# Three transposes of each batch by 32x32 blocks on VectorE and moves by DMA, in a two-layer graph network

## Chip, cores and metric

One core of one Trainium2 chip. The metric is the device time of one execution in microseconds (us); a quoted time is the median of three or more executions unless the text says "one look". "Waits" and "half clock" come from the one profiled execution of each kernel.

## The reference, cut to what matters

Thirty-two batches, each with x (512x512), a weighted adjacency matrix (512x512) and a node mask (512), all in fp32.

```python
# layer 0
h = relu(layernorm(x))
agg = (adj @ h) / max(rowsum(adj), 1e-6)
x = x + relu(concat([h, agg], -1) @ W.T)
# layer 1
h = relu(layernorm(x))                       # "h1" in this text
q, k = split(h @ Wqk);  v = h @ Wv
w = scale * mask * sum(q * (adj @ (k * mask)), -1)
x = x + softmax(w)[:, None] * v
```

## The kernel before

Per batch it computes five products on TensorE: y = h W2, out = h W1 + A y (a double one), z = A (h1 masked), q = h1 M with M = Wq Wk^T, and v = h1 Wv. Each product of 512x512 matrices is done with seven products of halves instead of eight (a Strassen scheme), so the left and the right operand need a few sums first; the class `Left` makes those of the left operand. The kernel hands TensorE the left operand transposed, so h, the adjacency and h1 are each transposed once a batch, by TensorE against an identity, through PSUM, with a ScalarE copy back:

```python
class Left:                                  # sums of the left operand, on VectorE
    def __init__(self, t, name, tag):
        s = big.tile([P, 3, 2, H], F32, tag=tag, bufs=1, name=f"{name}_s")
        a11, a12, a21, a22 = block(t, 0, 0), block(t, 1, 0), block(t, 0, 1), block(t, 1, 1)
        s1, s2, s4 = s[:, 0], s[:, 1], s[:, 2]
        tt(s1, a21, a22, ALU.add)
        tt(a21, a11, a21, ALU.subtract)
        tt(s2, s1, a11, ALU.subtract)
        tt(s4, a12, s2, ALU.subtract)
        self.p = {1: a11, 2: a12, 3: s4, 4: a22, 5: s1, 6: s2, 7: a21}

def transpose_block(dst, src, c, func, name):
    p = ps_t.tile([P, 4, P], F32, tag="t", name=name)
    for d in range(4):
        nc.tensor.transpose(p[:, d, :], src[:, ts(d, P)], ident)
    nc.scalar.activation(dst[:, :, ts(c, P)], p, func)

def transpose_h1(b):                         # h and the adjacency alike
    t = tile4("h1T", 1, f"h1T_{b}")
    for c in range(C):
        transpose_block(t, XN[1, b][:, c, :], c, AF.Relu, f"pt1_{b}_{c}")
    H1T[b] = Left(t, f"h1T_{b}", "h1Ts")

# ... (layer_norm: statistics and the normalization on VectorE; the products; the softmax) ...

for i in range(B + 1):
    between = []
    if i < B:
        layer0_y(i)
    if i > 0:
        transpose_h1(i - 1)
        mask_h1(i - 1)
        XN.pop((1, i - 1))
        layer1_z(i - 1)
    if i < B:
        transpose_adj(i)
    if i + 1 < B:
        load_a(i + 1)
        XN[0, i + 1] = layer_norm(i + 1, f"0_{i + 1}")
    if i > 0:
        between = layer1_q(i - 1)
    if i < B:
        layer0_out(i, between)
    # ...
    if i + 1 < B:
        transpose_h(i + 1)
        normalize_adj(i + 1)
    if i > 0:
        layer1_v(i - 1)
    if i + 2 < B:
        load_x(i + 2)
```

The loop is the order of the program's text. The framework that builds the kernel puts instructions of one engine into an order of its own that keeps their dependences; once the kernel is built, these lists are fixed.

## Time and profile before

| | before |
|---|---|
| median of three executions | 2618.34 us (2617.97 to 2618.83) |
| TensorE's share of the chain that ended last | 97% |
| one batch, from one y to the next | 79.9 us |
| of it the three transposes on TensorE | 5.5 us |
| VectorE busy | 1647.6 us, 63% |
| DMA engines busy, data queue | 11.7% |
| granted TensorE clock, mean | 0.999 |

The share of the chain says whose time counts. Busy shares of the other engines are only room. One line that the prediction uses in words, from the list of waits (who waited for whom, us in total, times, longest):

```profile
PE pv L103 <- DVE u3v L64: 22.5, 31, 0.8
```

TensorE loses 0.75 us a batch at the start of a part of v, because VectorE is late with a sum that reads PSUM.

### The profile page before, as it was taken

The numbers are of one execution on the slowest core, as the hardware profiler recorded it, in microseconds if no ns is written. First come the engines' busy times: TensorE is split into PE (matmuls) and PEld (weight loads), VectorE is DVE, ScalarE is ACT, GpSimd is POOL, SyncE is SP. The second block draws the span as 40 slices with busy tenths as digits, with TensorE's granted clock in tenths as the row PEclk, the third lists the DMA queues.
The fourth block names the chain that finished last, engine by engine and source line by source line (L and its number), as shares of the span: only waits on it lengthen the run. The fifth ranks groups of instructions, "written<-read, shape, count | busy, mean of one in ns | idle before, by whom it ended". The sixth has DMA issues, their size and how long they took to land.

```text
span 2616.5 us, 30420 instructions
## 1 busy us (share of the span) xinstructions
PE 2559.3 (98%) x12548; PEld 2218.6 (85%) x12548; DVE 1647.6 (63%) x3282; ACT 481.6 (18%) x854; POOL 74.3 (3%) x70
## 2 busy tenths in 40 slices
PE   6999999999999999999999999999999999999998
PEld 4888888888888888888888888888888888888887
DVE  4766567666576665676665766656766657666555
ACT  2211212111121112121111211121211112111211
POOL 0000000000000000000000000000000000000000
PEclk9999999999999999999999999999999999999999
DMA  4100111010111000110101110011101011100000
GB/s 146 33 33 30 35 49 49 33 49 17 49 49 49 33 33 33 49 49 33 49 17 49 49 49 33 33 33 49 49 33 49 17 49 49 49 33 33 33 17 33
DMA packets 53514, 107.91 MB, mean 41 GB/s; under 512 B 1632, under 2 KB 1632, under 8 KB 53376
## 3 DMA queue, kind: packets, MB, share of 16 engines
q1 hardware_dynamic: 53376, 105.98, 11.7%
q8 instruction: 98, 1.61, 0.3%
q14 instruction: 40, 0.33, 0.0%
HBM read 72.42 MB, written 33.55 MB: 41 GB/s over the span
## 4 chain that ended last, share of the span: by engine, by line
PE 97%; DVE 1%; DMA 0%; SPq 0%; ACT 0%; issue 0%; POOL 0%; POOLq 0%; DVEq 0%
PE po L103 30%; PE pz L103 15%; PE pq L103 15%; PE pv L103 15%; PE py L103 15%; PE pth L154 2%; PE pta L154 2%; PE pt L154 2%; DVE u3v L64 1%; PE pm L339 1%; DMA mask_sb<-in_nodemask_dram 0%; PE pbc L297 0%; DVE st L202 0%; SPq L181 0%; PE psum L307 0%
## 5 line engine op out<-in xcount | busy, mean ns | idle before, releaser
L103 PE MATMUL po<-w1T,hT 128*128 128x256 f32 x768 | 200.5, 383 | 0.0
L103 PE MATMUL po<-y,aT 128*128 128x256 f32 x768 | 197.1, 379 | 0.0
L103 PE MATMUL pv<-wv_sb,h1T 128*128 128x256 f32 x768 | 186.7, 379 | 0.0
L103 PE MATMUL pq<-m_sb,h1T 128*128 128x256 f32 x768 | 186.6, 379 | 0.0
L103 PE MATMUL pz<-h1m,aT 128*128 128x256 f32 x768 | 186.6, 379 | 0.0
L103 PE MATMUL py<-w2T,hT 128*128 128x256 f32 x768 | 181.7, 379 | 0.7 <-ACT s1y L121 0.7
L202 DVE BATCH_NORM_STATS2 st<-x 128x6 f32<-128x512 f32 x256 | 166.8, 674 | 9.6 <-DMA x<-in_x_dram 8.1
L208 DVE TENSOR_SCALAR xn<-x,mv,rstd 128x512 f32<-128x512 f32 x256 | 122.6, 543 | 66.3 <-POOL rstd L205 66.3
L103 PEld LDWEIGHTS py<-w2T,hT 128*128 128x128 f32 x768 | 145.7, 190 | 21.3 <-ACT s1y L121 1.1
L103 PEld LDWEIGHTS po<-y,aT 128*128 128x128 f32 x768 | 145.9, 190 | 19.8
L103 PEld LDWEIGHTS po<-w1T,hT 128*128 128x128 f32 x768 | 143.2, 190 | 18.6
L103 PEld LDWEIGHTS pv<-wv_sb,h1T 128*128 128x128 f32 x768 | 141.2, 190 | 16.7
L103 PEld LDWEIGHTS pq<-m_sb,h1T 128*128 128x128 f32 x768 | 141.1, 190 | 16.6
L103 PEld LDWEIGHTS pz<-h1m,aT 128*128 128x128 f32 x768 | 141.0, 190 | 16.6
L205 POOL TENSOR_TENSOR rstd<-rstd,mhalf 128x4 f32<-128x4 f32 x64 | 73.6, 1151 | 2488.5 <-DVE rstd L204 2488.5
L64 DVE TENSOR_TENSOR pre<-po,u2o 128x512 f32<-128x512 f32 x64 | 44.3, 692 | 149.9 <-PE po L103 149.9
L103 PE MATMUL po<-w_t,hT_s 128*128 128x256 f32 x512 | 131.5, 379 | 0.0
L103 PE MATMUL po<-y_t,aT_s 128*128 128x256 f32 x512 | 131.4, 379 | 0.0
L155 ACT ACTIVATE hT<-pth 128x512 f32<-128x512 f32 x128 | 69.8, 595 | 334.5 <-PE pth L154 334.4
L103 PE MATMUL pv<-wv_t,h1T_s 128*128 128x256 f32 x512 | 121.1, 379 | 0.0
L103 PE MATMUL pz<-h1m_t,aT_s 128*128 128x256 f32 x512 | 121.0, 379 | 0.0
L103 PE MATMUL pq<-m_t,h1T_s 128*128 128x256 f32 x512 | 121.0, 379 | 0.0
(151 smaller groups left out, 4389.3 us busy)
## 6 DMA issues: line engine op xcount, KB each, us to landing
x<-in_x_dram SPq DMA_DIRECT2D x32, 1024.0 KB, 5.3
adj<-in_adj_dram SPq DMA_DIRECT2D x32, 1024.0 KB, 5.2
out_dram<-x SPq DMA_DIRECT2D x32, 1024.0 KB, 4.3
w_in<-in_L_gnn_W_dram SPq DMA_DIRECT2D x2, 1024.0 KB, 9.0
w_in<-in_L_gnn_Wqk_dram SPq DMA_DIRECT2D x2, 1024.0 KB, 13.1
wv_sb<-in_L_gnn_Wv_dram SPq DMA_DIRECT2D x1, 1024.0 KB, 14.4
mask_sb<-in_nodemask_dram SPq DMA_DIRECT2D x1, 64.0 KB, 12.0
```

The costliest lines, as they stand in the source:

```text
L64: nc.vector.tensor_tensor(o, a, b, op=op)
L103: nc.tensor.matmul(bank[:, rc, :], left.p[k][:, dc, ts(rc, P)], right.p[k][:, dc, :], start=(first and n == 0), stop=(n == 4 * len(pairs) ...
L154: nc.tensor.transpose(p[:, d, :], src[:, ts(d, P)], ident)
L155: nc.scalar.activation(dst[:, :, ts(c, P)], p, func)
L202: nc.vector.bn_stats(st, X[b][:, c, :])
L205: nc.gpsimd.tensor_tensor(rstd, rstd, mhalf, op=ALU.pow)
L208: nc.vector.tensor_scalar(xn[:, c, :], X[b][:, c, :], mv[:, c, 0:1], rstd[:, c:c + 1], op0=ALU.subtract, op1=ALU.mult,)
L339: nc.tensor.matmul(p, wqT[:, a, ts(d, P)], wkT[:, a, :], start=(a == 0), stop=(a == D - 1))
```

## The change

Its intent is to take all three transposes off TensorE, the engine that sets the end. VectorE transposes the 32x32 blocks of a matrix in place. That leaves each block in the wrong quadrant of 32 partitions, and 16 DMA transfers put them where they belong: each moves one source quadrant of partitions into one target quadrant, 32 partitions with 16 runs of 128 bytes, 64 KB. Each 128x128 block is turned where it stands, so the products index their left operand the other way round (not shown in the diff). ScalarE now does the normalization together with the relu. To make room, the results of q and v are no longer stored and are combined straight from PSUM. The transposed h gets two buffers.

```diff
+    def turn(t, src, name, how):
+        if how == "pe":
+            for c in range(C):
+                transpose_block(t[:, c, :].rearrange("p (d n) -> p d n", d=4), src[:, c, :], f"{name}_{c}")
+            return
+        for c in range(C):
+            nc.vector.transpose(src[:, c, :], src[:, c, :])
+        s16, t16 = (u.rearrange("p c (d n) -> p (c d) n", n=P) for u in (src, t))
+        for q in range(4):
+            for r in range(4):
+                nc.sync.dma_start(out=t16[ts(q, 32), :, ts(r, 32)], in_=s16[ts(r, 32), :, ts(q, 32)])
 # ... layer_norm:
-        xn = tile4("xn", 2, f"xn{name}")
+        nb = small.tile([P, C], F32, tag="nb", name=f"nb{name}")
+        nc.vector.scalar_tensor_tensor(nb, mv[:, :, 0], -1.0, rstd, op0=ALU.mult, op1=ALU.mult)
+        h = tile4("h", 2, f"h{name}")
         for c in range(C):
-            nc.vector.tensor_scalar(
-                xn[:, c, :], X[b][:, c, :], mv[:, c, 0:1], rstd[:, c:c + 1],
-                op0=ALU.subtract, op1=ALU.mult,
-            )
-        return xn
+            nc.scalar.activation(h[:, c, :], X[b][:, c, :], AF.Relu, bias=nb[:, c:c + 1], scale=rstd[:, c:c + 1])
+        return h
 # ... transpose_h:
-        t = tile4("hT", 1, f"hT_{b}")
+        t = tile4("hT", 2, f"hT_{b}")
+        turn(t, HN.pop((0, b)), f"pth_{b}", "dma")
+        HT[b] = Left(t, f"hT_{b}", "hTs", 2)
 # ... transpose_adj (one buffer still):
+        turn(t, A.pop(b), f"pta_{b}", "dma")
 # ... transpose_h1, now with the masking in it:
+        h = HN.pop((1, b))
+        hm = tile4("h1m", 1, f"h1m_{b}")
         for c in range(C):
+            nc.vector.tensor_scalar(hm[:, c, :], h[:, c, :], mcol[:, c, b:b + 1], None, op0=ALU.mult)
         t = tile4("h1T", 1, f"h1T_{b}")
+        turn(t, h, f"pt1_{b}", "dma")
+        H1M[b] = Right(hm, f"h1m_{b}", big, "h1mt")
+        H1T[b] = Left(t, f"h1T_{b}", "h1Ts")
 # ... q and v: products of PSUM pieces with z, or added to x, in half-width pieces;
 #     temporaries from two buffers to one, the tiles "c" from three to two
```

More of the change, by code (lines that the diff above doesn't have):

```diff
@@ L66, with __init__ @@
     class Left:
-        def __init__(self, t, name, tag):
-            s = big.tile([P, 3, 2, H], F32, tag=tag, bufs=1, name=f"{name}_s")
-            a11, a12, a21, a22 = block(t, 0, 0), block(t, 1, 0), block(t, 0, 1), block(t, 1, 1)
+        def __init__(self, t, name, tag, bufs=1):
+            s = big.tile([P, 3, 2, H], F32, tag=tag, bufs=bufs, name=f"{name}_s")
+            a11, a12, a21, a22 = block(t, 0, 0), block(t, 0, 1), block(t, 1, 0), block(t, 1, 1)
             s1, s2, s4 = s[:, 0], s[:, 1], s[:, 2]
@@ L103, in part @@
                         nc.tensor.matmul(
-                            bank[:, rc, :], left.p[k][:, dc, ts(rc, P)], right.p[k][:, dc, :],
+                            bank[:, rc, :], left.p[k][:, rc, ts(dc, P)], right.p[k][:, dc, :],
                             start=(first and n == 0), stop=(n == 4 * len(pairs) - 1),
@@ L123, in product @@
         part(6, p6, True)
-        u2 = temp("u2", 2)
+        u2 = temp("u2", 1)
         tt(u2, p6, s1, ALU.add)
@@ L127, in product @@
         part(7, p7, True)
-        u3 = temp("u3", 2)
+        u3 = temp("u3", 1)
         tt(u3, p7, u2, ALU.add)
@@ L148, in store_in, with transpose_block @@
         return sink
-    def transpose_block(dst, src, c, func, name):
+    def transpose_block(dst, src, name):
         p = ps_t.tile([P, 4, P], F32, tag="t", name=name)
@@ L154, in transpose_block @@
             nc.tensor.transpose(p[:, d, :], src[:, ts(d, P)], ident)
-        nc.scalar.activation(dst[:, :, ts(c, P)], p, func)
-    X, A, XN, HT, AT, Y, H1T, H1M, Z, DEGM, SM = ({} for _ in range(11))
+        nc.scalar.activation(dst, p, AF.Copy)
+    def turn(t, src, name, how):
[9 more added lines that the diff above has]
+                nc.sync.dma_start(out=t16[ts(q, 32), :, ts(r, 32)], in_=s16[ts(r, 32), :, ts(q, 32)])
+    X, A, HN, HT, AT, Y, H1T, H1M, Z, DEGM, SM = ({} for _ in range(11))
     def load_x(b):
@@ L177 @@
     for half, tag, bufs in (
-        (w0[:, 0:F], "x", 3), (w0[:, F:2 * F], "x", 3), (wqk[:, 0:F], "c", 3), (wqk[:, F:2 * F], "c", 3),
+        (w0[:, 0:F], "x", 3), (w0[:, F:2 * F], "x", 3), (wqk[:, 0:F], "c", 2), (wqk[:, F:2 * F], "c", 2),
     ):
@@ L225, in transpose_h @@
     def transpose_h(b):
-        t = tile4("hT", 1, f"hT_{b}")
-        xn = XN.pop((0, b))
-        for c in range(C):
-            transpose_block(t, xn[:, c, :], c, AF.Relu, f"pth_{b}_{c}")
-        HT[b] = Left(t, f"hT_{b}", "hTs")
+        t = tile4("hT", 2, f"hT_{b}")
+        turn(t, HN.pop((0, b)), f"pth_{b}", "dma")
+        HT[b] = Left(t, f"hT_{b}", "hTs", 2)
     def transpose_adj(b):
         t = tile4("aT", 1, f"aT_{b}")
-        an = A.pop(b)
-        for c in range(C):
-            transpose_block(t, an[:, c, :], c, AF.Copy, f"pta_{b}_{c}")
+        turn(t, A.pop(b), f"pta_{b}", "dma")
         AT[b] = Left(t, f"aT_{b}", "aTs")
     def transpose_h1(b):
+        h = HN.pop((1, b))
+        hm = tile4("h1m", 1, f"h1m_{b}")
+        for c in range(C):
+            nc.vector.tensor_scalar(hm[:, c, :], h[:, c, :], mcol[:, c, b:b + 1], None, op0=ALU.mult)
         t = tile4("h1T", 1, f"h1T_{b}")
-        xn = XN[1, b]
-        for c in range(C):
-            transpose_block(t, xn[:, c, :], c, AF.Relu, f"pt1_{b}_{c}")
+        turn(t, h, f"pt1_{b}", "dma")
+        H1M[b] = Right(hm, f"h1m_{b}", big, "h1mt")
         H1T[b] = Left(t, f"h1T_{b}", "h1Ts")
-    def mask_h1(b):
-        t = tile4("h1m", 1, f"h1m_{b}")
-        xn = XN[1, b]
-        for c in range(C):
-            nc.vector.tensor_scalar(t[:, c, :], xn[:, c, :], 0.0, mcol[:, c, b:b + 1], op0=ALU.max, op1=ALU.mult)
-        H1M[b] = Right(t, f"h1m_{b}", big, "h1mt")
     def layer0_y(b):
-        y = tile4("c", 3, f"y_{b}")
+        y = tile4("c", 2, f"y_{b}")
         product(f"y_{b}", [(HT[b], w2)], store_in(y))
@@ L261, in sink @@
             if u is not None:
-                t = big.tile([P, 2, H], F32, tag="pre", bufs=2, name=f"pre_{b}_{r}{c}")
+                t = big.tile([P, 2, H], F32, tag="pre", bufs=1, name=f"pre_{b}_{r}{c}")
                 tt(t, p, u, ALU.add)
@@ L267, in layer0_out, with sink @@
         product(f"o_{b}", [(HT.pop(b), w1), (AT[b], Y.pop(b))], sink, between)
-        XN[1, b] = layer_norm(b, f"1_{b}")
+        HN[1, b] = layer_norm(b, f"1_{b}")
     def layer1_z(b):
-        Z[b] = tile4("c", 3, f"z_{b}")
+        Z[b] = tile4("c", 2, f"z_{b}")
         product(f"z_{b}", [(AT.pop(b), H1M.pop(b))], store_in(Z[b]))
     def layer1_q(b):
-        q = tile4("c", 3, f"q_{b}")
-        product(f"q_{b}", [(H1T[b], m)], store_in(q))
         z = Z.pop(b)
+        wc = small.tile([P, C, 2], F32, tag="wc", name=f"wc_{b}")
+        def sink(r, c, p, u):
+            t = big.tile([P, 2, H], F32, tag="pre", bufs=1, name=f"preq_{b}_{r}{c}")
+            if u is not None:
+                tt(t, p, u, ALU.add)
+                p = t
+            zb = block(z, r, c)
+            for rc in range(2):
+                nc.vector.scalar_tensor_tensor(
+                    t[:, rc, :], p[:, rc, :], 1.0, zb[:, rc, :], op0=ALU.mult, op1=ALU.mult,
+                    accum_out=wc[:, 2 * r + rc, c:c + 1],
+                )
+        product(f"q_{b}", [(H1T[b], m)], sink)
         w = small.tile([P, C], F32, tag="w", name=f"w_{b}")
-        for c in range(C):
-            nc.vector.scalar_tensor_tensor(
-                q[:, c, :], q[:, c, :], 1.0, z[:, c, :], op0=ALU.mult, op1=ALU.mult, accum_out=w[:, c:c + 1],
-            )
+        nc.vector.tensor_tensor(w, wc[:, :, 0], wc[:, :, 1], op=ALU.add)
         nc.vector.tensor_tensor(w, w, DEGM.pop(b), op=ALU.mult)
@@ L315, in layer1_v, with sink @@
     def layer1_v(b):
-        v = tile4("c", 3, f"v_{b}")
-        product(f"v_{b}", [(H1T.pop(b), w3)], store_in(v))
         xo, sm = X.pop(b), SM.pop(b)
-        for c in range(C):
-            nc.vector.scalar_tensor_tensor(
-                xo[:, c, :], v[:, c, :], sm[:, c:c + 1], xo[:, c, :], op0=ALU.mult, op1=ALU.add
-            )
+        def sink(r, c, p, u):
+            if u is not None:
+                t = big.tile([P, 2, H], F32, tag="pre", bufs=1, name=f"prev_{b}_{r}{c}")
+                tt(t, p, u, ALU.add)
+                p = t
+            xb = block(xo, r, c)
+            for rc in range(2):
+                k = 2 * r + rc
+                nc.vector.scalar_tensor_tensor(
+                    xb[:, rc, :], p[:, rc, :], sm[:, k:k + 1], xb[:, rc, :], op0=ALU.mult, op1=ALU.add
+                )
+        product(f"v_{b}", [(H1T.pop(b), w3)], sink)
         nc.sync.dma_start(out=out[b].rearrange("(c p) f -> p c f", p=P), in_=xo)
-    XN[0, 0] = layer_norm(0, "0_0")
+    HN[0, 0] = layer_norm(0, "0_0")
     mcol = const.tile([P, C, B], F32, name="mcol")
@@ L334 @@
         for c in range(4):
-            transpose_block(dst, t[:, c, :], c, AF.Copy, f"ptw_{dst.name}_{c}")
+            transpose_block(dst[:, :, ts(c, P)], t[:, c, :], f"ptw_{dst.name}_{c}")
     for d in range(D):
@@ L354 @@
             transpose_h1(i - 1)
-            mask_h1(i - 1)
-            XN.pop((1, i - 1))
             layer1_z(i - 1)
@@ L361 @@
             load_a(i + 1)
-            XN[0, i + 1] = layer_norm(i + 1, f"0_{i + 1}")
+            HN[0, i + 1] = layer_norm(i + 1, f"0_{i + 1}")
         if i > 0:
```

## The prediction

> **What bounds the kernel now.** I read the page first: busy time by engine, then the chain that ended last.
>
> ```profile
> PE 2559.3 (98%) x12548; PEld 2218.6 (85%) x12548; DVE 1647.6 (63%) x3282; ACT 481.6 (18%) x854; POOL 74.3 (3%) x70
> PE 97%; DVE 1%; DMA 0%; SPq 0%; ACT 0%; issue 0%; POOL 0%; POOLq 0%; DVEq 0%
> PE po L103 30%; PE pz L103 15%; PE pq L103 15%; PE pv L103 15%; PE py L103 15%; PE pth L154 2%; PE pta L154 2%; PE pt L154 2%; DVE u3v L64 1%; PE pm L339 1%; DMA mask_sb<-in_nodemask_dram 0%; PE pbc L297 0%; DVE st L202 0%; SPq L181 0%; PE psum L307 0%
> ```
>
> The reader is to see that the end is set by TensorE almost alone: five products (L103) make 90% of the chain, the three transposes of a batch (pth, pta, pt, L154) some 6.5%, and one wait for VectorE (u3v) 1%. Everything else is hidden. So TensorE time removed is time gained, unless the replacement makes TensorE wait.
>
> Next the groups by shape, for what one of each operation costs:
>
> ```profile
> L208 DVE TENSOR_SCALAR xn<-x,mv,rstd 128x512 f32<-128x512 f32 x256 | 122.6, 543 | 66.3 <-POOL rstd L205 66.3
> L154 PE MATMUL pth<-ident,xn 128*128 128x128 f32 x512 | 71.1, 283 | 0.2 <-ACT hT L155 0.2
> L154 PE MATMUL pt<-ident,xn 128*128 128x128 f32 x512 | 69.4, 278 | 1.2 <-DVE xn L208 1.0 <-ACT h1T L155 0.2
> L154 PE MATMUL pta<-ident,adj 128*128 128x128 f32 x512 | 69.3, 278 | 0.2 <-ACT wkT L155 0.2
> L155 ACT ACTIVATE hT<-pth 128x512 f32<-128x512 f32 x128 | 69.8, 595 | 334.5 <-PE pth L154 334.4
> L223 ACT ACTIVATE adj<-adj,rdeg 128x512 f32<-128x512 f32 x128 | 81.9, 711 | 7.3 <-DVE degm L221 5.9 <-DVE rdeg L219 1.4
> L64 DVE TENSOR_TENSOR u3o<-po,u2o 128x512 f32<-128x512 f32 x32 | 22.1, 692 | 84.3 <-PE po L103 84.3
> ```
>
> Busy time of 210 us for the transposes overstates them, because matmuls overlap. The timeline of one batch shows what a transpose holds TensorE for:
>
> ```profile
> 1239.92 1.04 PE L154 MATMUL pta<-ident,adj 128*128 128x128 f32 x8
> 1240.80 0.60 PE L103 MATMUL pq<-m_sb,h1T 128*128 128x256 f32 x2
> 1241.23 1.12 PE L154 MATMUL pta<-ident,adj 128*128 128x128 f32 x8
> 1242.19 1.46 PE L103 MATMUL pq<-m_sb,h1T 128*128 128x256 f32 x6
> 1242.42 0.37 SPq L165 DMA_DIRECT2D adj<-in_adj_dram  x1
> ```
>
> From start to start: 0.88 us for the first eight and 0.96 us for the second, 1.84 us a matrix, 5.5 us a batch. The same view has the starts of the products with y: 1214.08 and 1293.96, so a batch takes 79.9 us. A product of 56 matmul records lasts 12.1 us, the double one (out) 24.1, so the products are 72.4 us; transposes 5.5; the u3v wait 0.75 (22.5 us over 31 times in the list of waits); the rest, about 1.2, is the softmax's small matmuls.
>
> Last the DMA rows:
>
> ```profile
> q1 hardware_dynamic: 53376, 105.98, 11.7%
> x<-in_x_dram SPq DMA_DIRECT2D x32, 1024.0 KB, 5.3
> 5.78 2.45 SPq L165 DMA_DIRECT2D adj<-in_adj_dram  x1
> ```
>
> 11.7% of 16 engines over 2616.5 us is 4898 us for 53376 packets, 92 ns each. The issue of one megabyte (512 packets, 33 on each engine with the one that signals) holds the queue for 0.37 us when engines are free, and 2.45 us (third line) when they are backed up at the start; that is about the time the engines need to drain one. It then lands 5.3 us after the issue.
>
> **What the Trainium skill says.** (1) "DMA: Bandwidth & Descriptors", section "Why small descriptors are slow (HBM only)": transfers inside SBUF don't suffer the small-descriptor penalty; a packet costs its 32-byte beats and about 3 cycles more. The trace's own packet records fit that so far: 2048 bytes took 84 ns at the median, and the five of 64 bytes 8 ns each. No packet of 128 bytes between SBUF partitions is in this trace. (2) The same page, "Anatomy of one DMA": about 2 us fixed, mostly completion. The trace agrees: 5.3 us less 33 x 84 ns = 2.8 leaves 2.5. (3) "VectorE: DVE Perf Modes", "The three transpose paths": VectorE transposes 32x32 blocks only, 311 ns for 128x128 bf16. There is none in this trace; an ordinary one-result-per-cycle VectorE operation on 512 columns takes 692 ns here, and I take 0.69 us for a transpose of 128x512. The same section warns against plain strided DMA as a transpose; here the runs are 128 bytes, not single elements, so I don't apply its factor. (4) "ScalarE: Activation LUTs", "What ACT_TABLE_LOAD costs": 186 ns, 93 for each per-partition operand, 0.833 ns a column. One operand, 512 columns: 706; the trace has 711 (L223). With scale and bias both per partition I estimate 0.80 us.
>
> **The change part by part, for one batch.**
> *TensorE* loses 48 transposes: 5.5 us, x32 = 176 us. The transposes of the weights stay.
> *ScalarE* loses 12 copies out of PSUM (69.8/128 = 0.545 us each: 6.5) and two block copies of q and v (1.2), and gets 8 normalizations (8 x 0.80 = 6.4). From 481.6/32 = 15.1 to about 13.7 us; not a bound.
> *VectorE*, now 1647.6/32 = 51.5 us: less 8 normalizations (122.6/256 = 0.48 each: 3.8); plus 12 transposes x 0.69 = 8.3; q and v are now combined straight from PSUM in half-width pieces, 8 of about (256+151)/0.96 = 0.42 us in place of 4 of 0.65 to 0.70, plus accumulator reads: about 1.7; small ones 0.4. Sum 58 us, 79% of a 73.6 us batch: busier, not the bound by sum.
> *DMA* gets 3 x 16 moves of 64 KB, each 32 partitions x 16 runs of 128 bytes: again 512 data packets, 32 on an engine. By the two packet sizes above I estimate 10.5 ns for 128 bytes, so 33 x 10.5 = 0.35 us a move, about the 0.37 of an issue. SP: 48 x 0.37 = 18 us. Engines: 17 us plus 9.4 for the loads and stores (11.7% of 79.9), 36%. Not a bound.
> *Latency* of one transposed matrix: 16 x 0.37 + 2.5 = 8.4 us, then up to four Left additions of about 0.6 to 0.7 us. What hides it? For h there are now two buffers, and its input is ready a product or more ahead: hidden. For h1, its buffer comes free at the end of v and it is wanted at q, two products (24 us) later: hidden. The adjacency has one buffer: it can be written only after z has read the old one, and it is wanted after q, 12.1 us later, plus two matmuls of out. 8.4 us fits; the sums wanted by the second part of out come at 8.4 + 2.1 = 10.5, also in time. If an issue takes 0.65 us or more it no longer fits.
> The u3v wait may go too: in its stretch VectorE today is continuously busy behind the end of out, and the additions on h can now lie earlier: up to 0.75 x 31 = 23 us.
> Sum: 2618 - 176 = 2442; less up to 23 for u3v; plus some 10 us at both ends, where the h1 move of the last batch has less to hide behind; plus a stall of about 1 us a batch (32 us), because VectorE at 79%, working in order, will sometimes sit at an addition that waits for a move. About 2465 us.
>
> **The rivals.**
> *The adjacency window.* A packet of 25 ns instead of 10.5 makes a move 0.83 us, a matrix 13.2 + 2.5 = 15.7, and TensorE waits some 3 to 5 us a batch: 2540 to 2600. For it: no such packet is in the trace, and 16 engines read and write only 32 partitions at a time. Against: both small packet sizes are at 8 to 9 ns.
> *DMA as the bound.* 1584 packets an engine and batch overtake 73.6 us when one costs over (73.6 - 9.4)/1584 = 40 ns. At 60 ns a batch is 104 us and the kernel 3400. Or the moves aren't in flight together: if each waits for the one before (about 2.5 us), 16 take 40 us, a batch 120, and the kernel some 3900. For it: a new pattern with interleaved destinations. Against: the loads at the start were issued back to back.
> *VectorE takes TensorE's place.* Waiting in order at additions that depend on moves, it frees PSUM late and TensorE waits as at u3v, for more: 2 to 4 us a batch, 2510 to 2570. For it: 63% goes to 79%. Against: the whole out stretch, 24 us, leaves VectorE mostly idle (waits of 2.5 to 4.6 us for po).
>
> **Range and chances.** Smooth (up to 2500): about half. One of the mild rivals eating a third to most of the gain: 0.17 still faster by over 2% (below 2566), 0.13 within 2%. DMA-bound or serialized moves: 0.20, and then slower by a lot. Predicted 2465 us, 8 in 10 from 2420 to 2640: the upper end holds the adjacency window at its worst, the lower a hidden everything with u3v gone. Faster 0.67, same 0.13, slower 0.20.
>
> **What would show it.** Right: TensorE still over 95% of the chain, its busy time lower by about 210 us, transposes on VectorE near 0.69 us each, moves issued every 0.4 us, DMA share near 35%, no wait of TensorE for a move or an aT addition above 1 us a batch. Wrong: an issue of a move over 0.65 us or a landing over 5 us; DMA share above 80%; in the list of waits, po waiting for aT, or VectorE's additions waiting for aT or h1T; VectorE's transposes well over 0.69 us.

## The result, and the profile after

The changed kernel takes 2574.89 us (four executions, 2570.72 to 2576.42) against 2618.59 beside it. The ratio is 0.9831 (95% interval 0.9814 to 0.9848): 1.7% faster, where 5.9% was forecast. That is clear of the noise, but below the 2% from which the record calls a kernel faster. Here and below a ratio is the mean time of one kernel's runs over that of the other's runs of the same rounds, so it is not quite the ratio of the quoted medians. Executions over 1.5% slower than the fastest of the same kernel are left out of the means.

From the page of the changed kernel, the engines' busy time and the chain that ended last:

```profile
PE 2425.6 (94%) x11012; PEld 2088.7 (81%) x11012; DVE 1815.2 (71%) x3890; ACT 422.0 (16%) x662; POOL 65.2 (3%) x70
PE 71%; DVE 12%; SPq 9%; DMA 4%; issue 2%; ACT 1%; POOL 0%; DVEq 0%; POOLq 0%
PE po L104 30%; PE pq L104 15%; PE pv L104 14%; SPq L170 8%; PE py L104 8%; DVE h L166 4%; PE pz L104 2%; DMA h1T<-h 2%; DVE h1T_s L64 1%; DVE z L64 1%; DVE y L64 1%; DMA x<-in_x_dram 1%; DVE st L217 1%; DVE u3y L64 1%; DVE h1T L64 1%
```

Before, TensorE made 97% of the chain. Now it is 71%, and half of the rest is one path: the queue that issues the moves (SPq L170, 8%), VectorE's transposes (h, L166, 4%) and the landing of the moves (h1T<-h, 2%), that is, the time from an issue until its data are in place. The kernel is no longer bound by TensorE alone. TensorE's busy time fell by 133.7 us, not by the 210 of the forecast.

From the groups of instructions of the changed kernel (busy us, mean ns of one; then the idle time before them and what ended most of it):

```profile
L225 ACT ACTIVATE h<-x,nb,rstd 128x512 f32<-128x512 f32 x256 | 187.7, 803 | 678.6 <-DVE nb L222 648.8
L104 PE MATMUL pq<-m_sb,h1T 128*128 128x256 f32 x768 | 197.0, 402 | 50.0 <-DMA h1T<-h 50.0
L166 DVE STREAM_TRANSPOSE h<-h 128x512 f32<-128x512 f32 x256 | 169.2, 691 | 27.3 <-ACT h L225 27.3
```

The new operations cost what was expected: 803 ns a normalization, 691 ns a transpose. But the matmuls of q rose most, from 379 to 402 ns here and to 433 ns in the group that reads h1T_s, and they have idle time in front of them. The list of waits of the changed kernel:

```profile
PE pq L104 <- DVE h1T_s L64: 54.7, 26, 2.8
PE pq L104 <- DMA h1T<-h: 50.0, 30, 3.0
```

q waits for the transposed h1 to land (30 of 32 batches, 1.7 us each) and then, in its second part, for VectorE's additions on it (26 batches, 2.1 us each). Nothing waits for the adjacency, beyond 0.6 us once.

Why is h1 late? One batch in the middle, first ScalarE's timeline (start, duration, what; in brackets the idle time before it and what ended it), then VectorE's, then the DMA queue's:

```profile
1192.70 2.93 ACT L225 ACTIVATE h<-x,nb,rstd 128x512 f32<-128x512 f32 x4 [19.04 <-DVE nb L222]
```

```profile
1201.52 0.71 DVE L166 STREAM_TRANSPOSE h<-h 128x512 f32<-128x512 f32 x1
...
1202.72 1.88 DVE L166 STREAM_TRANSPOSE h<-h 128x512 f32<-128x512 f32 x3
...
1218.20 0.71 DVE L166 STREAM_TRANSPOSE h<-h 128x512 f32<-128x512 f32 x1 [0.88 <-ACT h L225]
...
1221.19 0.69 DVE L166 STREAM_TRANSPOSE h<-h 128x512 f32<-128x512 f32 x1
1221.80 0.65 DVE L64 TENSOR_TENSOR h1T_s<-h1T 128x512 f32<-128x512 f32 x1
```

```profile
1204.67 0.59 SPq L170 DMA_DIRECT2D h1T<-h  x1
1205.36 0.56 SPq L176 DMA_DIRECT2D x<-in_x_dram  x1
1205.97 12.86 SPq L170 DMA_DIRECT2D h1T<-h  x15
```

ScalarE has h1 ready at 1195.6. VectorE, busy without a pause with the sums of v and y, the additions on hT and the four maskings, finishes the four transposes only at 1204.6. Then the queue needs 13.5 us for the sixteen moves with the load of the next x between them, 0.6 us or more each: the sixteenth is issued at 1218.2. The load's part in this can be read off the single issues: most moves follow each other after 0.67 us, and the sixteen of the adjacency right behind them take 10.70 us in all, but four of the moves behind the load hold the queue for 0.82, 0.82, 2.17 and 1.55 us. The last move lands 2.1 us after its issue, at 1220.3. On TensorE's timeline:

```profile
1216.25 1.89 PE L104 MATMUL pz<-h1m,aT_s 128*128 128x256 f32 x8
1220.73 3.62 PE L104 MATMUL pq<-m_sb,h1T 128*128 128x256 f32 x8 [2.60 <-DMA h1T<-h]
1224.19 1.89 PE L104 MATMUL pq<-m_t,h1T_s 128*128 128x256 f32 x8
```

q was due at 1218.1 and begins 2.6 us late. And the first eight matmuls after the gap take 3.62 us instead of 1.89. The busy time by stretches of this kernel shows why (stretch, its length, busy time of PE, PEld, DVE, ACT and POOL with instructions, granted TensorE clock, DMA share, GB/s):

```profile
1216.00:1220.00 4.00, 2.14 (x10) 1.53 (x9) 1.97 (x4) 2.65 (x4) 1.01 (x1) 1.00 0.63 100
1220.00:1224.00 4.00, 3.27 (x8) 2.62 (x9) 3.93 (x8) 0.28 (x1) 0.00 (x0) 0.58 0.65 98
```

The clock granted after the gap is 0.58 over the stretch. The clock records of the trace show 22 stretches at half speed, 82.5 us in all: 20 within the batches, all but one of 3.41 us (that one of 6.83), and one at each end. Before there was one, 6.3 us at the end. Half speed costs half of the stretch where TensorE works through it: (82.5 - 6.3) / 2 = 38 us. The Trainium skill, "TensorE: Matmul & The Clock Gate", section "Part 1: The HAM clock gate", says that the clock halves after an idle window of about 3.4 us and comes back after a busy one, and that these windows run free of the kernel. The trace agrees on the window: all 20 stretches begin on one grid of 3.413 us. But a window need not be idle throughout. In the window just before each stretch TensorE was idle for 1.9 to 2.7 us; no stretch began after a window with less, and the longest idle time in a window without one behind it was 1.96 us. (The ends of matmuls are modelled, so this is not sharp; and it holds for this kernel: in x_late, where single small matmuls lie in the gaps, 1.6 us was enough.) So it counts how a gap lies on the grid, and not its length alone: a gap of 2.07 us within one window (at 829.0) brought the half clock, one of 2.81 us that was cut into 1.41 and 1.40 us (at 1690.3) did not. Gaps of 1.9 to 3.0 us brought it in 20 of 32 batches.

Note VectorE's order in the same timeline: h1T landed at 1220.3, but the first addition on it ran at 1221.80, because the four transposes of the *next* batch's h, which had waited for ScalarE, stand ahead of it in VectorE's list, with two sums of z among them. (In this batch the second part of q did not wait for it, because the first part ran slow.)

The account: 2618.6 - 176 (the transposes) - 23 (the wait for u3v, which is gone) = 2420 would be the time with everything new hidden. Add 50.0 + 54.7 of waits and 38 of half clock: 2563. The other 12 us are not accounted for.

### The profile page after: what moved, and what is told of

The parts are those of the page before. It is cut to its first block, busy times and chain, and to the rows that moved or that the text cites. A ratio compares the mean times of both kernels' runs of the same rounds, so it can differ in the third digit from the quotient of the medians.

```text
span 2574.2 us, 30504 instructions
## 1 busy us (share of the span) xinstructions
PE 2425.6 (94%) x11012; PEld 2088.7 (81%) x11012; DVE 1815.2 (71%) x3890; ACT 422.0 (16%) x662; POOL 65.2 (3%) x70
## 3 DMA queue, kind: packets, MB, share of 16 engines
q1 hardware_dynamic: 864384, 206.74, 38.9%
## 4 chain that ended last, share of the span: by engine, by line
PE 71%; DVE 12%; SPq 9%; DMA 4%; issue 2%; ACT 1%; POOL 0%; DVEq 0%; POOLq 0%
PE po L104 30%; PE pq L104 15%; PE pv L104 14%; SPq L170 8%; PE py L104 8%; DVE h L166 4%; PE pz L104 2%; DMA h1T<-h 2%; DVE h1T_s L64 1%; DVE z L64 1%; DVE y L64 1%; DMA x<-in_x_dram 1%; DVE st L217 1%; DVE u3y L64 1%; DVE h1T L64 1%
## 5 line engine op out<-in xcount | busy, mean ns | idle before, releaser
L225 ACT ACTIVATE h<-x,nb,rstd 128x512 f32<-128x512 f32 x256 | 187.7, 803 | 678.6 <-DVE nb L222 648.8
L104 PE MATMUL pq<-m_sb,h1T 128*128 128x256 f32 x768 | 197.0, 402 | 50.0 <-DMA h1T<-h 50.0
L104 PEld LDWEIGHTS pq<-m_sb,h1T 128*128 128x128 f32 x768 | 153.6, 203 | 84.0 <-issue 58.4
L104 PE MATMUL pq<-m_t,h1T_s 128*128 128x256 f32 x512 | 144.5, 433 | 54.7 <-DVE h1T_s L64 54.7
L166 DVE STREAM_TRANSPOSE h<-h 128x512 f32<-128x512 f32 x256 | 169.2, 691 | 27.3 <-ACT h L225 27.3
L104 PEld LDWEIGHTS pq<-m_t,h1T_s 128*128 128x128 f32 x512 | 108.2, 217 | 83.3 <-issue 65.3
L104 PE MATMUL py<-w_t,hT_s 128*128 128x256 f32 x512 | 122.7, 383 | 6.9 <-DVE hT_s L64 6.9
L220 POOL TENSOR_TENSOR rstd<-rstd,mhalf 128x4 f32<-128x4 f32 x64 | 64.5, 1008 | 2453.1 <-DVE rstd L219 2453.1
```

What stands on the lines that cost most here:

```text
L104: nc.tensor.matmul(bank[:, rc, :], left.p[k][:, rc, ts(dc, P)], right.p[k][:, dc, :], start=(first and n == 0), stop=(n == 4 * len(pairs) ...
L166: nc.vector.transpose(src[:, c, :], src[:, c, :])
L220: nc.gpsimd.tensor_tensor(rstd, rstd, mhalf, op=ALU.pow)
L225: nc.scalar.activation(h[:, c, :], X[b][:, c, :], AF.Relu, bias=nb[:, c:c + 1], scale=rstd[:, c:c + 1])
```

## The experiments

The theory after reading the result, A: h1's path (VectorE's transposes, 16 issues, landing, additions) is longer than its window. Rivals: that the adjacency, or VectorE's load as such, or contention of the DMA engines costs the time. For each kernel the diff is against the changed kernel. "Half clock" is the total of half-speed stretches (6.3 us before the change). In the column of waits, "landing" is q's wait for the moves of h1 to land and "additions" its wait for VectorE's sums on h1T (h1T_s); u3y and s1z are partial sums of the products y and z.

| kernel | median us | ratio to before | waits of TensorE that matter, us | half clock, us |
|---|---|---|---|---|
| changed | 2574.89 | 0.9831 | landing 50.0, additions 54.7 | 82.5 |
| h1_pe | 2479.44 | 0.9469 | none at q | 12.8 |
| adj_pe | 2678.73 | 1.0232 | additions 113.7, ScalarE's aT 20.3 | 113.2 |
| h_pe | 2546.14 | 0.9724 | additions 32.8, aT_s 19.5 | 8.9 |
| all_pe | 2633.07 | 1.0055 | ScalarE's aT 36.9 | 6.6 |
| twice | 2781.45 | 1.0621 | landing 271.9 | 312.6 |
| x_late | 2556.44 | 0.9763 | additions 31.6, top 50.7 | 52.7 |
| h1_act | 2661.27 | 1.0165 | s1z 157.2 | 196.1 |
| warm | 2549.74 | 0.9738 | none at q | 11.6 |
| early | 2761.67 | 1.0550 | landing 14.9, additions 209.1, x 15.1 | 263.7 |
| actmask | 2570.36 | 0.9818 | landing 9.3, additions 81.0 | 98.4 |
| early_actmask | 2674.19 | 1.0208 | landing 7.6, additions 134.7, u3y 11.5 | 205.6 |
| one | 2510.98 | 0.9589 | landing 56.2, additions 3.8 | 42.3 |
| one_actmask | 2474.49 | 0.9450 | landing 13.4, additions 18.0 | 11.7 |
| one_early_actmask | 2507.51 | 0.9574 | landing 12.9, additions 39.0, u3y 11.7 | 14.7 |
| one_actmask_x | 2525.74 | 0.9646 | additions 33.5, top 44.7 | 30.0 |
| one_actmask_xact | 2472.33 | 0.9440 | landing 6.3, additions 23.8 | 14.9 |

### Which of the three transposes costs it

Each of the first three kernels puts one transpose back on TensorE, the fourth all three. A transpose on TensorE costs 1.84 us a batch, 59 us in all, so moving one off TensorE pays if the waits that it brings are below 59 us.

```diff
# h1_pe
-        turn(t, h, f"pt1_{b}", "dma")
+        turn(t, h, f"pt1_{b}", "pe")
# adj_pe
-        turn(t, A.pop(b), f"pta_{b}", "dma")
+        turn(t, A.pop(b), f"pta_{b}", "pe")
# h_pe
-        turn(t, HN.pop((0, b)), f"pth_{b}", "dma")
+        turn(t, HN.pop((0, b)), f"pth_{b}", "pe")
# all_pe: all three
```

> The changed kernel with h1 alone turned by TensorE again; h and the adjacency still by VectorE and moves. Theory (the h1 moves come too late for q, and that is the only place where TensorE waits): TensorE gets 59 us more work, but the waits for h1T (50 us) and for the addition h1T_s (55 us) go, and with them the half-clock stretches (about 39 us): about 2490 us, granted clock above 0.995. Rival (the queue of moves as a whole is too slow, the wait only changes its place): TensorE then waits for aT or hT and the time is 2550 us or more.

> The adjacency alone turned by TensorE. Theory: its moves stand behind those of h1 in the queue, so the waits at q stay (about 100 us and the half clock): 59 us more work, 2600 to 2640 us. Rival (the total of moves in the queue is what delays h1T): the waits at q shrink by half or more, and the time is below 2560 us.

> h alone turned by TensorE. Theory: the moves of h come after those of h1 and of the adjacency, a product before their use; taking them away helps only by 2.8 us a batch of VectorE work: waits at q mostly stay, 2590 to 2640 us. Rival (VectorE's backlog of transposes delays h1T): waits at q fall by more than half, below 2570 us.

> All three turned by TensorE, the rest of the change kept (ScalarE normalizes, q and v combined from PSUM, two buffers for hT). Theory: no waits at q, granted clock 0.999, TensorE has its 176 us back: 2590 to 2620 us, so the rest of the change is worth under 1%. Rival: the rest of the change costs by itself (half-width VectorE operations, ScalarE normalizing): above 2640 us.

With h1 alone back on TensorE the kernel takes 2479.44 us, 95 us *less* than with all three moved, although TensorE has 59 us more to do. That is 2420 + 59 to within a microsecond. Its chain, from its page:

```profile
PE 97%; DVE 1%; DMA 1%; SPq 0%; ACT 0%; issue 0%; POOL 0%; POOLq 0%; DVEq 0%; ACTq 0%
```

TensorE is the bound again and nothing waits at q: the transposes of h and of the adjacency are fully hidden, and all of the loss is h1's.

With the adjacency back instead, the kernel is slower than before, 2678.73 us, worse than I had expected. Its list of waits:

```profile
PE pq L104 <- DVE h1T_s L64: 113.7, 31, 3.8
```

The wait for the landing has shrunk to 3.3 us, once; the one for the additions has doubled. In one batch VectorE's timeline has the additions on aT, which had waited for ScalarE's copies, from 1185.43, and those on h1T behind them, from 1188.09. So the issue time is not the whole story, and VectorE's order is a second cause. With h back, 2546.14 us against an expected 2590 to 2640, a miss; the rival's forecast (waits down by more than half, below 2570) came true. There VectorE has no transposes of the next h to put ahead of the additions, and the waits for them are down to 32.8 us, 1.0 each. This spoke for VectorE's order as well, without proving it; the runs with one buffer below do that.

All three back on TensorE gives 2633.07 us, 0.5% slower than before. The rest of the change (normalization on ScalarE, the straight combination of q and v) therefore brings nothing on its own. It takes away the wait for u3v (22.5 us) and brings one of 36.9 us for ScalarE's copies of aT; 2420 + 176 + 37 is 2633.

### What the moves cost, and what the gap costs

Four kernels ask whether the sixteen issues, the load of x among them, or the half clock after the gap are what they seem.

```diff
# twice: each move of h1 cut in two, so 32 transfers of half the bytes
-    nc.sync.dma_start(out=t16[ts(q, 32), :, ts(r, 32)], in_=s16[ts(r, 32), :, ts(q, 32)])
+    for k in ((slice(0, 8), slice(8, 16)) if name.startswith("pt1") else (slice(0, 16),)):
+        nc.sync.dma_start(out=t16[ts(q, 32), k, ts(r, 32)], in_=s16[ts(r, 32), k, ts(q, 32)])
# x_late: the load of x behind the moves of h1
             transpose_h1(i - 1)
+            if i + 1 < B:
+                load_x(i + 1)
 ...
-        if i + 2 < B:
-            load_x(i + 2)
# h1_act: the moves of h1 issued from ScalarE
-        turn(t, h, f"pt1_{b}", "dma")
+        turn(t, h, f"pt1_{b}", "dma", nc.scalar)
# warm: four idle matmuls after z and four after q's first part
+        warm(f"warmz_{b}", hm.p[4][:, 0, :])
-        product(f"q_{b}", [(H1T[b], m)], sink)
+        product(f"q_{b}", [(H1T[b], m)], sink, [lambda: warm(f"warmq_{b}", H1T[b].p[1][:, 0, :])])
```

> The moves of h1 cut in two: 32 transfers of 32 KB in place of 16 of 64 KB, same bytes and same 128-byte packets. Theory (a transfer costs a fixed 0.6 us of issue, whatever it carries): h1T lands some 10 us later, TensorE waits 9 us a batch more and runs the clock down each time: 2830 to 2950 us. Rival (packets or bytes set the pace): within 20 us of 2575, or faster, since the first half can start before the last transposes.

> The changed kernel with one thing moved: the load of the next x (one megabyte) is issued behind the sixteen moves of h1 instead of between the first and the second. Theory (the moves of h1 reach q late because they are held up in the one queue; the load costs 0.6 us of issue and two moves behind it then wait 2.5 us more for the engines): h1T lands some 3 us earlier, the wait for its landing goes, of the 2.3 us for h1T_s under 1 us stays, and TensorE keeps its full clock: 2430 to 2490 us. Rival (the load is harmless, VectorE's late transposes alone set the start): 2550 us or more.

> The moves of h1 issued from ScalarE's queue, all else as in the changed kernel. Theory (the issue on SP, 0.67 us a move and in a row with the load, is the limit): with two queues h1T lands about 1 to 3 us earlier and the time is 2450 to 2540 us, unless ScalarE's own copies of z stand behind the issues. Rival (what limits is shared by both queues): a move takes longer on both when they overlap and the time stays above 2560 us.

> Useless matmuls put into the two gaps at q: four after z, four after the first part of q (1.7 us each), so that TensorE never idles there for long. Theory (a gap of 2 to 4 us makes the clock fall to one half for 3.4 us, which costs about 39 us in all): granted clock 0.998 or more, no matmul at half speed, and 2575 less 39 plus at most some 20 us for matmuls that overshoot the gaps: 2535 to 2565 us. Rival (the half clock has another cause than the gap): clock stays at 0.985, time 2575 us or more.

*twice*: 2781.45 us, the expected direction, less in size. The queue's timeline:

```profile
948.62 20.99 SPq L171 DMA_DIRECT2D h1T<-h  x30
```

Thirty transfers of half the bytes take 0.70 us each: the number of transfers sets the time, not their bytes. The landing wait went from 50.0 to 271.9 us, 8.5 us a batch.

*x_late*: 2556.44 us against 2430 to 2490. The landing wait is gone, as expected, but another took its place:

```profile
PE ptop L308 <- DVE top L303: 50.7, 29, 2.1
```

With x loaded later, VectorE takes its statistics later (it waits 25.3 us in all for x, 8.3 in the changed kernel). In one batch they and the transposes of that h lie at 1213.96 to 1223.7, among the sums of q, and the maximum over the batch's scores (top), which the softmax needs between q and out, comes late. The load no longer disturbs one path and is too late for another.

*h1_act*: 2661.27 us, slower than before. ScalarE's timeline shows what the rule of the Trainium skill, "DMA: Bandwidth & Descriptors", section "Rules for kernel authors", leaves out when it says that spreading transfers over several engines only saves issue time:

```profile
1237.87 13.92 ACTq L170 DMA_DIRECT2D h1T<-h  x16
1251.89 0.60 ACT L122 ACTIVATE s1z<-pz 128x512 f32<-128x512 f32 x1 [15.43 <-DMA h1T<-h]
```

Most of these issues took 0.64 us; with two of about 2 us, shortly after the load of x on the other queue, the average is 0.87 in this batch. ScalarE's copy of the first part of z stood behind all sixteen, so TensorE waited for it 157.2 us in all, and its half clock rose to 196.1 us.

*warm*: 2549.74 us, as expected (2535 to 2565). The idle matmuls fill the gaps and take 3.45 us a batch themselves, yet 25 us are gained. Waits at q are gone and half clock is down from 82.5 to 11.6 us. This shows that the slow matmuls after the gap are a cost of their own, not an artefact of the records.

The last kernel of this group measures the issue alone: behind the loop its program has six groups of four transfers into scratch tiles, one look.

```diff
# probe, the first and last two groups of six
+    for r in range(4):
+        nc.sync.dma_start(out=e1[0:32, :, ts(r, 32)], in_=s16[32:64, :, ts(r, 32)])         # as is
+    # ... 8 runs in place of 16; runs of 64 bytes; the source in HBM ...
+    for r in range(4):
+        nc.sync.dma_start(out=e2[:, 0:4, ts(r, 32)], in_=s16[:, 4:8, ts(r, 32)])            # 128 partitions, 4 runs
+    for r in range(4):
+        nc.sync.dma_start(out=e2[:, 8+2*r:10+2*r, 0:64], in_=s16[:, 8+2*r:10+2*r, 64:128])  # 128 partitions, 2 runs of 256 B
```

> Six groups of four transfers at the end, for the issue time by shape: the move as it is; the same with 8 runs in place of 16; with 64-byte runs; with 128-byte runs from HBM; 128 partitions with 4 runs of 128 bytes; 128 partitions with 2 runs of 256 bytes. Theory A (the issue time is the making of packets, one after the other): 8 runs take clearly less than 16 (0.3 to 0.45 us against 0.6), 64-byte runs as much as 128-byte runs. Theory B (fixed cost of a transfer inside SBUF): 8 runs take 0.55 us or more. If 32 partitions as such are the cause, the 128-partition group with as many packets takes 0.37 us like a load.

From the view of the scratch tile (issue time ns min/median/max; first and last start us), the move as it is, the one with 8 runs, and the one with 128 partitions and 2 runs:

```profile
L406 SPq DMA_DIRECT2D pd<-psrc x4: 585/627/632, 2540.4 to 2542.4; - x4
L408 SPq DMA_DIRECT2D pd<-psrc x4: 608/610/632, 2543.1 to 2545.1; - x4
...
L416 SPq DMA_DIRECT2D pd<-psrc x4: 619/623/639, 2551.2 to 2553.2; - x4
```

In all six groups the median issue is 0.61 to 0.64 us, whatever the number of runs, the bytes, the partitions or the source. The framework placed the groups into the work on the last batches (the one with the source in HBM at 2435 us, five from 2540 to 2554), but no other transfer was issued among them. So for these shapes it is a fixed cost of a transfer, and not contention with other transfers. It is no constant of the queue: a load or store of one megabyte that is issued alone takes 0.37 to 0.44 us in the same traces, and the load of x, issued right behind a move, 0.56 (median of 32 in the changed kernel; 0.37 before). What makes the difference was not found.

### VectorE's order

If the additions wait behind other work, VectorE should be relieved ahead of them, or made to do h1's transposes sooner.

```diff
# actmask: the four maskings of h1 on ScalarE
-            nc.vector.tensor_scalar(hm[:, c, :], h[:, c, :], mcol[:, c, b:b + 1], None, op0=ALU.mult)
+            nc.scalar.activation(hm[:, c, :], h[:, c, :], AF.Copy, scale=mcol[:, c, b:b + 1])
# early: masking and transposes of h1 right after its normalization in the program's text
             layer0_out(i, between)
+            prepare_h1(i)              # the maskings and nc.vector.transpose of h1, taken out of transpose_h1
# early_actmask: both
```

> The four maskings of h1 go from VectorE to ScalarE (idle for 84%), order as in the changed kernel. Theory (VectorE's backlog between the end of out and the transposes of h1): 1.9 us less before them, the waits at q shrink by about 2 us a batch and fewer clock falls: 2480 to 2540 us. Rival (the queue of moves alone matters): within 10 us of 2575.

> The 32x32 transposes and the masking of h1 are written in the program right behind the normalization, ahead of the last work of v and y on VectorE; nothing else changes. Theory (part of the lateness of h1T at q is that VectorE comes to its transposes late, 6 us after ScalarE has h1 ready): the moves of h1 start some us earlier and the waits at q shrink: 2480 to 2550 us. Rival (VectorE is full in this stretch, and what goes ahead pushes u3y or u3v back by as much): 2560 us or more, with TensorE waiting for u3y or u3v.

> Both together. Theory: moves of h1 start 4 us or more earlier, no wait at q over 1 us, clock 0.998: 2430 to 2490 us, at or below the version with h1 on TensorE (2479). Rival as for the first: TensorE waits for u3y or u3v instead, above 2530 us.

All three missed. *actmask* (2570.36 us) cut the landing wait from 50.0 to 9.3 us, but the wait for the additions rose from 54.7 to 81.0. In *early* (2761.67) and *early_actmask* (2674.19) the landing wait fell too, to 14.9 and 7.6 us, and the kernel got slower than before. VectorE's timeline of early_actmask says why:

```profile
852.94 2.83 DVE L167 STREAM_TRANSPOSE h<-h 128x512 f32<-128x512 f32 x4 [0.28 <-ACT h L226]
855.69 0.65 DVE L64 TENSOR_TENSOR h1T_s<-h1T 128x512 f32<-128x512 f32 x1
```

and TensorE's:

```profile
857.81 3.75 PE L104 MATMUL pq<-m_t,h1T_s 128*128 128x256 f32 x8 [4.76 <-DVE h1T_s L64]
```

h1T had landed by 851.2, when the first part of q began without a wait. The four additions could have begun then, but the four transposes of the next batch's h, released by ScalarE at 852.9, stand ahead of them, and the second part of q waits 4.76 us. h1 on its way sooner gains nothing while its additions have that place in VectorE's list.

Why slower, though? The next h has a chain of its own: the result of a batch is stored, its tile is then loaded with a new x, statistics, normalization, transposes. The queue's timeline of early:

```profile
1199.00 0.39 SPq L356 DMA_DIRECT2D out_dram<-x  x1
1199.43 2.04 SPq L171 DMA_DIRECT2D h1T<-h  x2
1203.46 0.37 SPq L177 DMA_DIRECT2D x<-in_x_dram  x1
```

The load goes out once the store has landed (4.4 us after its issue at the median). From the store to the end of the next h's transposes it takes 21.8 us in the changed kernel (1200.05 to 1221.88) and 21.8 in early (1199.00 to 1220.77). But the store comes 5.7 us after the end of v in the changed kernel and 10.6 us after it in early, since VectorE now does h1's maskings and transposes ahead of the last sums of v. So the additions on h1T, tied behind that chain, come 4.9 us later by the measure of TensorE's work; a batch of early is 187 / 32 = 5.8 us longer. Sooner for h1 was later for the next h, and with the order as it is, the later of the two counts.

### The second buffer of h

What puts the next batch's h ahead of the additions? The tile `h` has two buffers, so ScalarE can normalize the next h while the moves still read h1. With one buffer the next h has to wait until h1's moves are done, so its transposes can't come before h1T has landed. That is a buffer *less*.

```diff
# one
-        h = tile4("h", 2, f"h{name}")
+        h = tile4("h", 1, f"h{name}")
# one_actmask: and the maskings on ScalarE;  one_early_actmask: and prepare_h1
```

> One buffer for the normalized h in place of two, nothing else: the next h can then be normalized and turned only when the moves of h1 have read the old one, so VectorE gets the additions on h1T ahead of the transposes of the next h. Theory (the second half of the wait at q is VectorE's order: it stands at transposes that wait for ScalarE's h while h1T has landed): the wait for h1T_s falls from 55 us to under 35 us, that for the landing stays near 50: 2530 to 2560 us. Rival (the wait for h1T_s is only the landing plus three additions): no change beyond 10 us, or slower because the next h comes late.

> One buffer for h, and the maskings on ScalarE. Theory (both parts count: moves that start late, additions that stand behind transposes): landing wait under 15 us, wait for h1T_s under 40 us, clock 0.995 or more: 2460 to 2520 us. Rival (order of VectorE does not matter): as the masking alone, 2560 us or more.

> One buffer for h, maskings on ScalarE, and the transposes of h1 ahead of the rest of v and y. Without the one buffer this was 2674 us, with 135 us of waiting for h1T_s although h1T had landed. Theory: that wait falls to under 30 us and the time to 2430 to 2500 us. Rival (the early transposes push u3y and the rest back, and that is the cost): above 2600 us again.

*one* takes 2510.98 us (ratio 0.9589, 0.9575 to 0.9603), 64 us less than with two buffers and better than expected. VectorE's timeline of it:

```profile
1189.04 0.69 DVE L64 TENSOR_TENSOR h1T_s<-h1T 128x512 f32<-128x512 f32 x1 [1.83 <-DMA h1T<-h]
...
1190.97 0.70 DVE L166 STREAM_TRANSPOSE h<-h 128x512 f32<-128x512 f32 x1
```

The additions now begin as soon as h1T lands, three of the four ahead of the transposes of the next h, since ScalarE now normalizes that h only when the moves of h1 are done (its wait for them rose from 29.8 to 133.5 us). The wait for the additions fell from 54.7 to 3.8 us, the one for the landing stayed (56.2). That separates the two causes. With 20 us less of half clock, (82.5 - 42.3) / 2, the sum is 65 us, the gain measured. *one_actmask* adds the cure for the landing and reaches 2474.49 us, as expected (2460 to 2520). Its list of waits:

```profile
PE pq L104 <- DVE h1T_s L64: 18.0, 27, 1.1
PE pq L104 <- DMA h1T<-h: 13.4, 11, 2.5
```

At 5.5% faster than before (ratio 0.9450, 0.9436 to 0.9465) it beats both kernels. It agrees with the forecast's 2465, but only with two edits that the change doesn't have. *one_early_actmask* comes to 2507.51 us, just outside the expected 2430 to 2500. What counts is the comparison: with two buffers the same kernel took 2674.19, so the one buffer alone is worth 167 us there.

Two last kernels ask whether the load of x among the moves is worth anything now. One puts it behind the moves, as in x_late, the other issues it from ScalarE:

```diff
# one_actmask_xact
-        nc.sync.dma_start(out=X[b], in_=x[b].rearrange("(c p) f -> p c f", p=P))
+        nc.scalar.dma_start(out=X[b], in_=x[b].rearrange("(c p) f -> p c f", p=P))
```

> The best version so far (one buffer for h, maskings on ScalarE, 2474 us) with the load of x behind the moves of h1. Theory: the last waits at q (13 us for the landing, 18 us for the additions) go, but the statistics of the next x then fall on VectorE into q, as in the run with the late load alone, and the softmax's maximum comes late: a wait for top of about 1.7 us a batch, 2480 to 2520 us. Rival (only the moves matter): 2440 to 2465 us.

> The same best version with the load of x issued at its old time, but from ScalarE's queue. Theory: the moves of h1 lose only the issue of the load (0.4 to 0.6 us) and its gap on SP, they still share the engines with it; x comes when it came before, so no wait for top: 2450 to 2475 us. Rival (sharing the engines with the load is all of its cost): within 5 us of 2474.

*one_actmask_x*: 2525.74 us, 51 slower than one_actmask. The wait for top is back with 44.7 us over 29 times, as in x_late. *one_actmask_xact*: 2472.33 us, 2 us off one_actmask and hardly apart from it. So the load's place in the queue is worth next to nothing once the rest is right, while its lateness costs.

**What stays open.** About 50 us between the best kernels with all three transposes moved (2474 and 2472) and the 2420 at which everything would be hidden: of one_actmask's 54, 31 are the two waits shown and 3 half clock, and 20 aren't accounted for. (The 59 of h1_pe are its transposes.) What makes these issues 0.6 us and a lone load's 0.4. Whether fewer and larger transfers would shorten the path: only more and smaller ones were tried.

## Why the prediction was wrong

Forecast were 5.9%, measured 1.7%. That the time fell inside the range was luck: the working does not lead to it.

- **TensorE is the bound, and its transposes are 176 us: right.** h1_pe shows it to within a microsecond, since two of three transposes gone and hidden is 2479. One of its signs of being right, 210 us less busy time, went against its own working: 210 adds up overlapping matmuls, which hold TensorE for 176. Measured were 134 less; half clock in q, about 38, is most of the difference to 176. (The two starts 1214.08 and 1293.96 that it quotes stand in no view; y begins at 1213.91 and 1293.80, 79.9 us apart as well.)
- **Costs of the new operations: right.** Transpose 691 ns (0.69 forecast), normalization 803 ns (0.80), a half-width piece 0.42 us in q and 0.48 in v (0.42), VectorE 1815 us or 56.7 a batch (58), 71% of the span (79% of a shorter batch).
- **DMA as the bound: rightly put aside.** The data queue took 38.9% of the engines (36%). A packet of 128 bytes took 13.0 ns at the median of the trace's packet records, not 10.5. That doesn't matter at this share.
- **The wait for u3v: right**, it is gone, but in all_pe as well, so by the rest of the change and not by the moves.
- **The step that failed:** "For h1, its buffer comes free at the end of v and it is wanted at q, two products (24 us) later: hidden." The window was right: v ends at 1194.4, q is due at 1218.1, 23.7 us later. Two terms were mis-sized. First, the start: the sum lets the moves begin as soon as the buffer is free, but VectorE did the transposes only at 1204.6, 10.2 us into the window, because its list has the sums of v and y, additions and maskings first. Second, "16 x 0.37 + 2.5 = 8.4 us": an issue of such a move takes 0.59 to 0.63 us and the next follows after 0.67, and with the load among them the sixteen took 13.5 us. 10.3 + 13.5 + 2.1 landing + 0.4 start is 26.3 us, 2.6 more than the window. The duration 0.37 was a load's of another shape; the prediction says itself that at 0.65 us it no longer fits, but applied that only to the adjacency.
- **The rival named, the adjacency window: wrong place.** I looked for the tight window at the buffer that is single and rewritten latest. It had slack (no wait above 0.6 us). The rival's slow packets did not come either (13.0 ns, not 25). The issue of over 0.65 us, which the sum of the latency names as the limit, struck at h1 (one every 0.67 us).
- **The rival "VectorE takes TensorE's place": half right, and too small in the sum.** I put 1 us a batch for VectorE sitting "at an addition that waits for a move". The opposite happened: the additions had their data and sat behind the transposes of the next h. They cost 54.7 us, 1.7 us a batch. The reason I gave against it, that VectorE is mostly idle during out, held before the change (busy 8.2 of 25.0 us) but was of no use: in the batch shown, h1's transposes come in y, where VectorE was busy for 11.5 of 11.5 us, and its additions at the start of q, where it was busy for 3.93 of 4.00. An average of 71% said nothing of that.
- **A term that was missing:** the half clock after a gap, 38 us.

In sum: the forecast allowed 32 us for stalls and 10 for the ends, 42. Measured were 104.7 of waits, 38 of half clock and 12 of the rest, 155. The difference, 113, is the miss of 110 us but for rounding (the forecast's terms add up to 2461, and it says about 2465).

## What to carry to other kernels

When work leaves the bound engine for a path of several steps (an engine, sixteen issues, a landing, additions), add up the path in the timeline from the moment the first step *can run on its busy engine* until the consumer is due, and not from the moment a buffer is free; and take an issue's time from a transfer of the same shape, or measure it. Look at what stands ahead of the critical instruction in its engine's fixed list. A second buffer that lets later work start sooner can put that work ahead, and here one buffer less was worth 64 us. A short wait of TensorE may cost more than its length (here 38 us of half clock after 105 us of waits), so look at the granted clock just after it.

## What the Trainium skill lacked or had wrong

- "DMA: Bandwidth & Descriptors": for how long one issue holds the queue I found only a count of sequencer cycles for one plain instruction of earlier generations, with no dependence on the shape of the transfer or on what stands ahead of it. Here it is 0.59 to 0.64 us for transfers of short runs, whatever their bytes (probe), 0.37 to 0.44 us for a lone load of a megabyte, 0.56 us for one behind a move, and 0.64 us as a rule from ScalarE's queue, during which ScalarE does nothing else (h1_act). Its fixed time for one DMA is fitted to transfers issued from GpSimd; for those from SyncE the landing was 2.3 us at the median for the moves of h1.
- The same page, "Why small descriptors are slow (HBM only)": beats of 32 bytes and about 3 cycles. For 128 bytes between SBUF partitions I had read 10.5 ns off the other sizes; the records show 13.0 ns at the median, 13.6 in the mean.
- "TensorE: Matmul & The Clock Gate", section "Part 1: The HAM clock gate": half clock after an idle window of about 3.4 us. Here the grid of windows agrees (3.413 us), but 1.9 to 2.7 us of idle time within a window were enough, in 20 of 32 batches (1.6 us in x_late). The warning of its section "Why this matters for your kernels" against gaps of over about 3 us is therefore too lenient for this kernel, where gaps of 1.9 to 3.0 us did it.
- "VectorE: DVE Perf Modes", section "The three transpose paths": no figure for fp32. A 128x512 fp32 transpose by 32x32 blocks takes 691 ns here. No run here tests the factor in its warning against a plain strided DMA as a transpose; with runs of 128 bytes the moves, loads and stores together took 38.9% of the engines.
